# A two-layer transformer kernel in hi/lo float32: P^T one head longer in DRAM, and K and Q of a layer-1 head pair in one 512-column projection

## The chip, the core and the metric

The kernel runs on one core of one Trainium2 chip. The metric is device time in microseconds (us), lower is better. It is given as the median of three runs; one further execution was taken with the hardware profiler, and all rows below are from that one.

Engine names in the profile: PE is the matmul array (TensorE), PEld its weight loads, DVE is VectorE, ACT is ScalarE, POOL is GpSimd, SP is SyncE, whose queue issues all DMAs here.

## What is computed

Two transformer layers on x of shape (2, 512, 512), all in float32. Layer 0: attention with 32 query heads of width 128 that share 8 K/V heads, rotary embedding and a causal mask, then a feed-forward that is one linear map with eight low-rank additions. Layer 1: attention with 32 heads, biases, and a root-mean-square norm on Q and K, without a mask, then a gated feed-forward with low-rank additions. Every block is wrapped as x = x + LN(block(LN(x))):

```python
# layer 1 attention
q = rmsnorm((x @ Wq + bq).reshape(b, n, H, HD), gq)
k = rmsnorm((x @ Wk + bk).reshape(b, n, H, HD), gk)
v = (x @ Wv + bv).reshape(b, n, H, HD)
scores = einsum('bnhd,bmhd->bhnm', q, k) / sqrt(HD)
out = einsum('bhnm,bmhd->bnhd', softmax(scores), v) @ Wo + bo
```

## The kernel before

**Exact products from pairs.** Each float32 operand of a matmul is split into a high and a low part of the type fp32r (hi is a copy, lo = x - hi), and `mm3` adds three products: hi hi, hi lo, lo hi. So each operand costs a copy (ScalarE or VectorE) and a subtraction (GpSimd or VectorE), and each product three matmuls.

**Units and heads.** The work of a layer is cut into units: a head pair p of one batch b. A unit has two heads (j = 0, 1); the list `heads` numbers them. For each head TensorE has: the scores (four query tiles of 128 x 512), the product with V (`av`), and shares of the unit's projections of Q, K and V and of the output projection (`out_proj`, accumulated into y in SBUF).

**Order of issue.** The program is written out by a list scheduler that runs while the program is built. The items of TensorE stand in streams: `main` (scores and, for other units, attention products), "a" (attention products), "q", "v", "o" (fills: Q/K projections, V projections, output projections). Each item has a nominal place `nom` in `main` and a condition; `streams` takes a fill when its place has come, or, up to `ahead` places early, when `main` waits. The work of the other engines hangs on the items as generators, whose stages are issued when a modelled clock says so; `pick` gives an operation to the engine that would finish it first by fixed costs. On the chip each engine then runs its instructions in that order, held by semaphores. Since every instruction passes through one helper, all of them bear line 102 in the profile: they are told apart by tile names and shapes.

**Memory.** The large tiles share an arena of 37 slots of 4 KB a partition ("ar" in the profile); a tag (W for weights, P, T, PT, pt, qk, ot, v, nat, ...) takes a half or a whole slot, and `NBUF`, changed by `PHASES` at five places of the work, bounds how many of a tag may live. `room` says whether a tile fits; `wait` is a stage that waits for it, first come first served. PSUM tiles are ps_pj (projections), ps_s (scores), ps_oy (attention and output products), ps_tr (transposes).

**P^T.** In most units (`lag`) P is transposed not by TensorE but as 32 x 32 blocks on VectorE into T (in `softmax_tail`), stored to DRAM (pc in layer 0, pd in layer 1) and read back by four DMAs into PT with the blocks in place; from PT a copy and a subtraction make the pieces pt (hi, lo) of 256 queries by 128 keys, which `av_items` consumes. DRAM has three such buffers; the products of a head stand in `main` one head after its scores. The K and Q of a layer-1 unit are transposed in the same way through DRAM (`flip`; kdk and kdq).

**Layer-1 projections.** `l1_weights` loads Wk and Wq of a head pair each in two halves into two W tiles (hi, lo). `proj` makes, for K and then for Q, four row tiles of 128 x 256; two of them share a PSUM tile, to which VectorE adds the bias. A square (ScalarE) and a sum (VectorE) give the norm; K is scaled by it, and Q's factor rq is applied in the exponential:

```python
nc.vector.tensor_reduce(m, ps, AX.X, ALU.max, negate=True)
nc.vector.tensor_tensor(mr, m, r, ALU.mult)
```

**Weights ahead.** `LEAD` says how many units before its use a weight starts to load. Units near the ends of a layer (`CUT`) run batch by batch with weights of their own.

Of the kernel before, what the change touches and what calls it, by code (L numbers as in the profile page):

```python
# [30 lines left out]
LAT = 0.1  # L31
FIRST = "x0 x1 x2 k x3 q r v y o z"
# [24 lines left out]
class Item:  # L57
    """a piece of TensorE's work, to be issued when cond holds"""
# [5 lines left out]
class Engine:  # L64
    """An engine that keeps its order of issue, with a clock (us) of its work."""
# [58 lines left out]
class Engines:  # L124
    WEIGHT = dict(vector=1.0, scalar=0.5, gpsimd=0.0)

    def pick(self, *cands):
        """issue the one of the candidates (engine, op, args...) that is done first"""
# [21 lines left out]
    def mul(self, out, a, s):  # L150
        """by a factor of each row"""
        self.pick(("gpsimd", "tensor_scalar", out, a, s, 1.0, ALU.mult, ALU.mult),
                  ("vector", "tensor_scalar", out, a, s, None, ALU.mult),
                  ("scalar", "activation", out, a, AF.Copy, dict(scale=s)))

    def copy(self, out, a):
        """from PSUM"""
# [9 lines left out]
class Kern:  # L167
    """Work is written as items: functions, or generators that yield the time
    (of TensorE's work) after which their next stage is to be issued."""
# [3 lines left out]
                m=6, mr=6, rs=6, ri=6, st=6, mv=10, ve=8, r=10, c=8, r8=6, rq=4,  # L173
# [43 lines left out]
    # the large tiles: a half or the whole of a slot each (halves of one type only in a slot)  # L217
# [3 lines left out]
    def room(self, tag, n, dt=None):  # L221
        if self.live.get(tag, 0) + n > self.NBUF[tag]:
            return False
        free = sum(not u for u in self.used)
        if self.HALF[tag] == 2:
            return n <= free
# [69 lines left out]
    def phase(self, i):  # L296
        """what is tuned for each phase of the work"""
# [27 lines left out]
    def wait(self, tag, n=1):  # L325
        """in a stage: until n slots are free, first come first served"""
# [7 lines left out]
    def low(self, eng):  # L334
        """in a stage of low priority: until the engine has nothing issued to it"""
# [9 lines left out]
    def streams(self, main, fills, bg):  # L345
        """Issue the streams of items, each in its order: a fill when its nominal place in
        main has come, or main waits; bg starts at its nominal place."""
# [30 lines left out]
    def pe(self, t):  # L378
        """t: at the full clock, which TensorE has after a busy tick only"""
# [13 lines left out]
    def mm3(self, out, pairs, start=True, stop=True):  # L393
        """exact hi/lo products: hi hi + hi lo + lo hi"""
# [11 lines left out]
    def setup(self):  # L406
# [10 lines left out]
        self.pd0 = [[self.dr.tile([P, 4, 2, 64 * (h + 1)], F32, name=f"pc{i}{h}") for h in range(2)] for i in range(3)]  # L417
        self.pd = [self.dr.tile([P, 2, 4, 256], F32, name=f"pd{i}") for i in range(3)]
        self.kd = {n: [self.dr.tile([P, 4, 256], F32, name=f"kd{n}{i}") for i in range(2)] for n in "kq"}
        self.ready = {}  # L420
        self.ident = cp.tile([P, P], F32, name="ident")
# [7 lines left out]
    def consts(self):  # L429
# [5 lines left out]
        nc.vector.scalar_tensor_tensor(self.g, self.gqk[:, 0:1], SCALE, self.gqk[:, 1:2], ALU.mult, ALU.mult)  # L435
# [6 lines left out]
    def split(self, hi, lo, raw):  # L442
        """hi + lo = raw exactly"""
# [105 lines left out]
    def resid(self, b, tt, lvl):  # L549
        """x of level lvl + 1 = x + LN(y); returned short of a constant of each row"""  # L550
# [10 lines left out]
        if lvl == 3:  # L561
# [10 lines left out]
            nc.sync.dma_start(self.xsrc(b, tt, 4), x)  # L572
            self.rel(x)
# [6 lines left out]
        def store():  # L580
# [8 lines left out]
            nc.sync.dma_start(self.xsrc(b, tt, lvl + 1), xo)  # L589
            self.rel(xo)  # L590
# [3 lines left out]
    def boundary(self, b, tt, lvl):  # L594
        """from the finished y of level lvl on"""
# [21 lines left out]
    def out_proj(self, b, first, last, ot, w, badd, lvl):  # L617
        """y += O Wo over the heads of this unit"""
# [415 lines left out]
    def l1_pre(self, hp, b, w, lag):  # L1034
# [4 lines left out]
        def proj(i, n, tt):  # L1039
# [11 lines left out]
            if z == 0:  # L1051
                return
# [630 lines left out]
```

## Time and profile before

| | |
|---|---|
| median of 3 runs | 2111.2 us (2106.71 to 2113.66) |
| span of the profiled execution | 2117.8 us (no time of that execution beyond its span is listed) |
| mean granted TensorE clock | 0.993 |
| TensorE busy | 2056.7 us, 97% |
| VectorE, GpSimd, ScalarE busy | 1801.4, 1446.3, 1337.7 us |
| DMA | 370.54 MB, mean 175 GB/s |
| instructions | 41211 |

By stage, from the windows: layer 0's attention runs to about 650 us, layer 0's feed-forward and the norms around it to about 750, layer 1's attention to about 1890, layer 1's feed-forward to the end. "Busy" of an engine is the time in which at least one of its instructions was under way; matmuls overlap, so one that is listed with 283 ns follows the one before it much sooner. The chain of work that ended last merges runs of instructions, and the length of such a run divided by its count is the step from one matmul to the next.

### The profile page before, as it was taken

To read this page: it belongs to the slowest core of one execution; us is meant where nothing else is said; L and a number is where in the kernel's file an instruction comes from. 1 tells how busy PE (TensorE), PEld (TensorE's weight loads), DVE (VectorE), ACT (ScalarE), POOL (GpSimd) and SP (SyncE) were. 2 spreads that over 40 slices of the span, in tenths; PEclk is the share of its full clock that TensorE was granted. 3 is DMA by queue.
4 is the path that set the end of the run, shared out by engine and by line. 5 is a ranking of instruction groups with operands and counts; after the bars stand their busy time and mean duration, and the time that the engine had idled before them with its cause. 6 is when DMAs were issued, how large, how long until landed. Compare 5 with 4: busy or idle time off the path is not lost.

```text
span 2117.8 us, 41211 instructions
## 1 busy us (share of the span) xinstructions
PE 2056.7 (97%) x12605; PEld 1827.5 (86%) x12605; DVE 1801.4 (85%) x4210; ACT 1337.7 (63%) x3247; POOL 1446.3 (68%) x1786
## 2 busy tenths in 40 slices
PE   8999999999999999999999999999999999989998
PEld 7888888888888798889899999999999898977886
DVE  7998899899888889889889999899989988888534
ACT  5776677577766668776666666666667666664212
POOL 5686678688875567877677777777777776774212
PEclk9999999999999999999999999999999999999999
DMA  2476567577652235887877777777777787763021
GB/s 98 127 183 166 145 185 183 143 200 199 177 159 66 71 103 166 244 232 223 227 202 229 220 227 211 207 221 219 225 206 232 213 240 212 224 178 93 31 67 44
DMA packets 476566, 370.54 MB, mean 175 GB/s; under 512 B 117400, under 2 KB 424488, under 8 KB 476344
## 3 DMA queue, kind: packets, MB, share of 16 engines
q1 hardware_dynamic: 476344, 367.91, 60.9%
q8 instruction: 99, 1.62, 0.3%
q14 instruction: 123, 1.01, 0.2%
HBM read 232.12 MB, written 135.66 MB: 174 GB/s over the span
## 4 chain that ended last, share of the span: by engine, by line
PE 54%; DMA 12%; DVE 9%; SPq 3%; issue 2%; POOL 2%; ACT 2%; DVEq 0%; ACTq 0%; POOLq 0%
PE ps_pj L102 23%; PE ps_oy L102 19%; PE ps_s L102 10%; DVE ar L102 6%; SPq L102 3%; DMA pd<-ar 3%; DMA ar<-pd 2%; POOL ar L102 2%; DMA kdk<-ar 2%; ACT ar L102 2%; DMA ar<-kdq 2%; DMA kdq<-ar 2%; PE ps_tr L102 1%; DMA ar<-pc 1%; DVE m L102 1%
## 5 line engine op out<-in xcount | busy, mean ns | idle before, releaser
L102 POOL TENSOR_TENSOR ar<-ar,ar 128x256 fp32r<-128x256 f32 (+4 forms) x1223 | 1058.3, 887 | 456.6 <-ACT ar L102 333.6
L102 PE MATMUL ps_oy<-ar,ar 128*128 128x256 f32 (+2 forms) x4014 | 832.2, 342 | 28.7 <-DVE ar L102 14.0
L102 PEld LDWEIGHTS ps_oy<-ar,ar 128*128 128x128 f32 x4014 | 653.5, 190 | 133.1 <-DVE ar L102 22.5
L102 ACT CAST ar<-ar 128x256 fp32r<-128x256 f32 (+3 forms) x1166 | 531.5, 490 | 305.4 <-DMA ar<-pd 117.1
L102 PE MATMUL ps_pj<-ar,xh 128*128 128x256 f32 (+1 forms) x3392 | 635.2, 285 | 0.9 <-POOL ar L102 0.6
L102 PEld LDWEIGHTS ps_pj<-ar,xh 128*128 128x128 f32 x3392 | 536.0, 190 | 14.5 <-POOL ar L102 1.1
L102 PE MATMUL ps_pj<-ar,xl 128*128 128x256 f32 (+1 forms) x1696 | 482.9, 285 | 0.0
L102 DVE STREAM_TRANSPOSE ar<-ar 128x256 f32<-128x256 f32 (+3 forms) x688 | 347.9, 533 | 16.9 <-DMA pd<-ar 9.7
L102 DVE TENSOR_TENSOR ar<-ps_pj,ar 128x512 f32<-128x512 f32 (+2 forms) x448 | 305.4, 683 | 52.5 <-PE ps_pj L102 44.8
L102 PE MATMUL ps_s<-ar,ar 128*128 128x512 f32 (+2 forms) x1252 | 338.5, 376 | 8.6 <-DVE ar L102 4.7
L102 PEld LDWEIGHTS ps_pj<-ar,xl 128*128 128x128 f32 x1696 | 322.9, 190 | 2.1 <-DVE xl L102 0.7
L102 PE MATMUL ps_pj<-xh,ar 128*128 128x512 f32 x816 | 286.6, 399 | 0.7 <-ACT xh L102 0.7
L102 DVE TENSOR_TENSOR y<-ps_oy,y 128x512 f32<-128x512 f32 x272 | 184.8, 680 | 81.8 <-PE ps_oy L102 80.2
L102 PEld LDWEIGHTS ps_s<-ar,ar 128*128 128x128 f32 x1252 | 214.5, 189 | 44.0 <-DVE ar L102 12.6
L102 DVE TENSOR_TENSOR ar<-ar,ar 128x256 fp32r<-128x256 f32 (+5 forms) x328 | 207.9, 652 | 51.1 <-ACT ar L102 50.1
L102 ACT ACTIVATE ar<-ps_s,mr,rq 128x512 f32<-128x512 f32 x256 | 198.6, 777 | 46.7 <-DVE mr L102 36.9
L102 PEld LDWEIGHTS ps_pj<-xh,ar 128*128 128x128 f32 x816 | 154.0, 189 | 31.7 <-ACT xh L102 1.1
L102 DVE TENSOR_REDUCE m<-ps_s 128x1 f32<-128x512 f32 x256 | 170.9, 673 | 6.2 <-PE ps_s L102 5.0
L102 ACT ACTIVATE ar<-ar,ri 128x512 f32<-128x512 f32 (+3 forms) x245 | 149.6, 621 | 38.3 <-DVE ri L102 37.1
L102 POOL TENSOR_SCALAR ar<-ar,ri 128x512 f32<-128x512 f32 (+3 forms) x202 | 133.0, 661 | 54.3 <-DVE ri L102 48.9
L102 PE MATMUL ps_pj<-xl,ar 128*128 128x512 f32 (+1 forms) x408 | 161.2, 395 | 0.0
L102 ACT ACTIVATE ar<-ps_s,m 128x512 f32<-128x512 f32 (+3 forms) x256 | 133.8, 526 | 23.4 <-DVE m L102 14.8
(91 smaller groups left out, 2105.5 us busy)
## 6 DMA issues: line engine op xcount, KB each, us to landing
pd<-ar SPq DMA_DIRECT2D x240, 256.0 KB, 3.7
ar<-pd SPq DMA_DIRECT2D x480, 128.0 KB, 3.3
ar<-pc SPq DMA_DIRECT2D x200, 128.0 KB, 3.0
ar<-in_wq SPq DMA_DIRECT2D x86, 256.0 KB, 4.1
ar<-in_wo SPq DMA_DIRECT2D x86, 256.0 KB, 3.6
kdk<-ar SPq DMA_DIRECT2D x31, 512.0 KB, 4.8
ar<-kdk SPq DMA_DIRECT2D x124, 128.0 KB, 4.0
kdq<-ar SPq DMA_DIRECT2D x31, 512.0 KB, 5.1
```

The source lines that it names most:

```text
L102: r = self.k.tc.keep_in_program_order(f(*args, **kw))
```

## The change

- P^T of a lagged unit is consumed two heads after its scores, not one (`pend`), the output projection one head later, and there are five DRAM buffers, not three. Layer 1's loads from DRAM and its copies out of PT keep the order of their use (`turn`, `place`); a head waits for its DRAM buffer's last reader (`loads`).
- K and Q of a layer-1 head pair have one weight array `wkq1` of 512 columns, loaded in four quarters, one bias array, and one matmul of 512 columns for each chunk and product. The items stand half a head earlier (`EARLY`). The norm's factors are made for two row tiles at a time.
- Layer-1 scores: g carries the sign, and one pass over the scores applies Q's factor and takes the minimum.
- `room` leaves two slots free when a W, v, nat or raw tile is asked for. The last feed-forward's weights wait until the last Wo is loaded (`wlast`). Two stores release their tile a stage later.
- Comments and docstrings are taken out. `PHASES` is as before; rq goes from 4 to 8.

```diff
+EARLY = 0.5
...
         free = sum(not u for u in self.used)
+        if tag in ("W", "v", "nat", "raw"):
+            free -= 2
...
-        self.pd0 = [... for i in range(3)]
-        self.pd = [... for i in range(3)]
+        self.pd0 = [... for i in range(5)]
+        self.pd = [... for i in range(5)]
...
+        head = st["head", j]
+        while self.loads.get(head - 5, 2) < 2:
+            yield 0.1
+        self.loads.setdefault(head, 0)
         yield from self.wait("T")
...
+        o = 1 - h if st["causal"] else h
+        while not st["causal"] and self.turn[0] < st["place", j] + o:
+            yield 0.1
         yield from self.wait("PT")
+        self.turn[0] = max(self.turn[0], st["place", j] + o + 1)
         pt = self.t("PT", [P, 4, 256])
         for b in range(4):
             nc.sync.dma_start(pt[32 * b:32 * b + 32, :, :n], d[:, b, :].rearrange("(a k) c -> k a c", a=4))
-        yield
+        self.loads[head] += 1
+        yield
+        while not st["causal"] and self.turn[1] < 2 * head + o:
+            yield 0.1
...
-            bqk = self.t("bqk", [P, 2, 256])
-            for i, n in enumerate(("bq", "bk")):
-                self.bcast(bqk[:, i, :], a[n][hp * 256:(hp + 1) * 256])
-        early = [bias] + [self.load_w(a["w" + n + "1"][hp], [P, NC, 256], w, n) for n in "kq"]
+            bkq = self.t("bqk", [P, 512])
+            self.bcast(bkq, a["bkq"][hp * 512:(hp + 1) * 512])
+        def quarter(c):
+            if c % 2 == 0:
+                yield from self.wait("W", 2)
+                box[c // 2] = (self.t("W", [P, 2, 512], F32R), self.t("W", [P, 2, 512], F32R))
...
+            self.nc.sync.dma_start(raw, a["wkq1"][hp][:, c:c + 1, :])
...
+            if box["n"] == NC:
+                w["kq"] = [box[0], box[1]]
+        early = [bias] + [lambda c=c: quarter(c) for c in range(NC)]
...
-            self.mm3(pj[:, z, :], [(self.xh[b][:, c, sl], self.xl[b][:, c, sl], w[n][0][:, c, :], w[n][1][:, c, :])
-                                   for c in range(NC)])
+            self.mm3(pj.rearrange("p n d -> p (n d)"),
+                     [(self.xh[b][:, c, sl], self.xl[b][:, c, sl], w["kq"][c // 2][0][:, c % 2, :], w["kq"][c // 2][1][:, c % 2, :])
+                      for c in range(NC)])
...
-            nc.vector.tensor_tensor(nat[:, ts, :], pj, bias, ALU.add)
+            for i, n in enumerate("kq"):
+                nc.vector.tensor_tensor(st["nat" + n][:, tt, :], pj[:, i, :], w["b"][:, i * 256:i * 256 + 256], ALU.add)
...
-            nc.scalar.activation(sq, nat[:, ts, :].rearrange("p t (h d) -> p (t h) d", h=2), AF.Square)
+            for i, n in enumerate("kq"):
+                nc.scalar.activation(sq[:, 2 * i:2 * i + 2, :], st["nat" + n][:, tt, :].rearrange("p (h d) -> p h d", h=2),
+                                     AF.Square)
...
-        early = [pq(1, "k", t) for t in range(4)] + [pq(0, "q", t) for t in range(4)]
+        early = [Item(lambda t=t: proj_ok(t), lambda t=t: proj(t)) for t in range(4)]
...
-            nc.vector.tensor_reduce(m, ps, AX.X, ALU.max, negate=True)
...
-            nc.vector.tensor_tensor(mr, m, r, ALU.mult)
...
-            yield from self.softmax_tail(st, j, qt, ps, mr, r, S)
+            nc.vector.tensor_scalar(ps, ps, r, 3.0e38, ALU.mult, ALU.min, accum_out=m)
+            yield
+            yield from self.softmax_tail(st, j, qt, ps, m, -1.0, S)
...
+                    while "o" not in self.wlast:
+                        yield 0.5
                     yield from self.wait("W", 2)
...
-            pre(n)[2]["slot", j] = i % 3
+            pre(n)[2]["slot", j] = i % 5
...
+                if n > 1 and lag[n - 2] and lag[n - 1]:
+                    fill["o"] += post(n - 2)
...
-                if n > 0 and lag[n - 1]:
+                if n and lag[n - 1] and not lag[n]:
                     fill["o"] += post(n - 1)
...
-            if i and lag[heads[i - 1][0]]:
-                todo += av_lag(*heads[i - 1])
+            while pend and (len(pend) >= 2 or not lag[n]):
+                todo += av_lag(*heads[pend.pop(0)])
+            if lag[n]:
+                pend.append(i)
...
-                    x.nom = x.nom or base + 2 + k * m / len(xs)
+                    x.nom = x.nom or base + 2 + k * m / len(xs) - (EARLY * m if L and f == "q" and len(xs) == 4 else 0)
```

## The prediction

> **What bounds the kernel now.** I read the page's engine shares and clock row first, then busy time by stage, then the chain of waits and the timeline of TensorE, last the groups by shape.
>
> Part 1 of the page and the clock row of part 2 (engine, busy us, share, instructions; one digit per 1/40 of the span):
>
> ```profile
> PE 2056.7 (97%) x12605; PEld 1827.5 (86%) x12605; DVE 1801.4 (85%) x4210; ACT 1337.7 (63%) x3247; POOL 1446.3 (68%) x1786
> PEclk9999999999999999999999999999999999999999
> ```
>
> TensorE is the bound: 61 us of the span are idle. So a change pays only by fewer TensorE microseconds or by filling some of those 61. The windows say where they are (window, length, PE busy, PEld, DVE, ACT, POOL, clock, DMA share, GB/s):
>
> ```profile
> 50.00:600.00 550.00, 544.59 (x2975) 475.02 (x2974) 489.60 (x1308) 380.06 (x1094) 411.17 (x494) 1.00 0.64 170
> 600.00:750.00 150.00, 144.52 (x796) 120.18 (x795) 126.24 (x321) 99.65 (x252) 94.74 (x125) 1.00 0.29 92
> 750.00:1050.00 300.00, 288.28 (x1933) 261.27 (x1933) 263.76 (x583) 211.53 (x466) 220.38 (x276) 0.99 0.68 200
> 1050.00:1700.00 650.00, 644.97 (x4530) 598.26 (x4529) 592.48 (x1315) 422.99 (x974) 486.72 (x587) 1.00 0.76 218
> 1700.00:1900.00 200.00, 186.04 (x1216) 169.47 (x1214) 168.04 (x384) 132.24 (x294) 147.41 (x184) 0.96 0.76 217
> ```
>
> Idle: 5.4 (layer 0), 5.5 (between the layers), 11.7 (start of layer 1), 5.0 (650 us of steady layer 1), 14.0 (its end). The rest lies in the first 50 us and after 1900, which the change hardly touches. VectorE, at 90% in steady layer 1, comes next.
>
> What those gaps are, in TensorE's timeline (start, length, instruction, count, idle before and what ended it):
>
> ```profile
> 1871.63 0.51 PE L102 MATMUL ps_oy<-ar,ar 128*128 128x256 f32 x2 [0.97 <-POOL ar L102]
> ...
> 1876.43 0.63 PE L102 MATMUL ps_oy<-ar,ar 128*128 128x256 f32 x2 [1.50 <-POOL ar L102]
> ```
>
> 256-column products into ps_oy are O^T = V^T P^T over a piece of P^T: TensorE waits until GpSimd has made its low part. In the waits of all engines ps_oy comes first on TensorE: 14.0 us on VectorE, 8.5 on GpSimd, 5.6 on ScalarE.
>
> The price of the projections, from the chain that ended last (start, length, count):
>
> ```profile
> 1328.10 2.88 PE ps_pj L102 x24
> 1500.72 2.87 PE ps_pj L102 x24
> 1911.56 2.72 PE ps_pj L102 x12
> 1944.85 2.78 PE ps_pj L102 x12
> 1959.91 2.77 PE ps_pj L102 x12
> ```
>
> The first two are K/Q pieces of 256 columns, 0.120 us each; the others 512-column products of the last stage, 0.227 to 0.232 us.
>
> **The change part by part.** *Projection.* One layer-1 unit (head pair, batch) now runs 4 row tiles x 4 chunks x 3 products for K and again for Q: 96 matmuls of 256 columns, 96 x 0.120 = 11.5 us. After: 48 of 512, by the middle piece 48 x 0.231 = 11.1 us. The saving, 0.44 us, times 32 units is 14 us, on the path, since steady layer 1 leaves TensorE 0.8% idle. The Trainium skill's page "TensorE: Matmul & The Clock Gate", section "Back-to-back issue gap", speaks against most of it: columns/2.4 plus 2.5 ns, so 109 and 216 ns, and a unit would save 0.13 us, 4 us in all. I take the trace's 14 and keep 4 as the weak end; 20, with the shortest 512 piece (2.72), is the other.
>
> *Scores of layer 1*, 256 of them: the maximum (673 ns) and its product with the row factor (365 ns) become one pass over PSUM that scales, writes back and reduces. No such instruction is in the trace; the nearest row is layer 0's masked reduction, 128x512, 700 ns, with its accumulator read, 137 ns. VectorE saves (1038-837) x 256 = 51 us; if it cost two full passes (1373 ns) it would lose 86, and if the read were free it would save 87. I take 51. The exponential loses its per-row scale: 777 to 686 ns (layer 0's row), 23 us of ScalarE.
>
> *Bias and squares*: 128 bias additions of 682 ns become 256 of half the size, by layer 0's 256-column row 415 ns: VectorE +19 us. 128 squares of 630 ns become 256 at about 402 (the 256-column cast): ScalarE +22 us. The sum reductions, the 64 reciprocal roots on GpSimd and the K scalings keep their count. Net VectorE -32 us, ScalarE 0. None of it is counted in the sum: TensorE covers it, and losing that cover (the two-pass case) would add 105 us over the 1100 of layer 1, VectorE would go from 91% to 100%, and some 15 us could be lost.
>
> *Weights*: 21 sets come as four quarters of 128x512 instead of four halves of 2x256; loads stay 84, and 42 bias loads become 21. Low parts: 168 GpSimd subtractions of 769 ns become 84 of 1309, -19 us of GpSimd. But projection now starts when all four quarters and both nat tiles are there; before, K needed its own two. The old set is released about half a head later (a layer-1 unit, two heads, takes 34 us: in the chain such a piece comes at 1466.87 and at 1500.72), which leaves about one head to load the next; a set's loads land in 4.1 to 4.6 us and its casts (0.6 us) and subtractions pipeline behind. Zero in the steady part.
>
> *P^T rests a head more.* Per head, 8 pieces (layer 1) or 5 (layer 0) are consumed one head later. Moved with them: the eight loads from DRAM, their casts and subtractions, and the output projection (by one head). On the SP queue the load is no longer issued at once behind the store: today SP stands 212.8 us, 105 times, on stores of pd, and weight loads and K/Q stores queue behind. ScalarE stands 117.1 us on the loads themselves, and casts, then GpSimd's subtractions, queue behind that. With a head of slack both should mostly go; they are not TensorE time. On TensorE I credit half of the attention gaps: the waits of each window put 5.1 us (layer 0), 8.4 (start of layer 1) and 11.1 (its end) on ps_oy, 24.6 together, so -12. Half, because a piece can only be cast when a pt slot (5 to 7) is free, so the extra time is in DRAM, not in finished pieces. Ends: 0 and -24.
>
> *The clock.* 1700-1900 shows 0.96, 8 us lost. The same page, section "What's actually happening", makes the clock fall only after an idle window of some 3.4 us; the longest wait of TensorE there is 2.2 us. By the page, shorter gaps change nothing; by the trace, a stretch rich in small gaps does lose clock, so fewer gaps recover some: -2 of the 8.
>
> *Fill.* The first head of each lagged stretch already has no attention product; now two have none. Layer 1: 24 x 0.12 = 2.9 us of TensorE work put off; layer 0 about 1.8, an estimate from the same step per column. If nothing fills in, +4.7; a head's VectorE work (0.91 x 17 = 15 us) exceeds what is left, so I take +3.
>
> *Longer lives.* V, Wo and full PT and pt slots stay a head longer in the same arena, weights must leave two slots free, P^T loads and casts keep an order, and the last feed-forward's weights wait for the last Wo. These waits are made while the program is written out: they move an instruction's place and hold up nothing by themselves on an engine's queue. K's chain (squares, root, scaling, transposes, 4.8 us to DRAM, 4.0 back, scaling, casts) starts when both projections end, later than now, but EARLY moves the projection half a head forward. Together between 0 and +40; I take +5, mostly for 1700-1900, where the last wait falls. Two small ends: four more zeroing DMAs (2.4 to 2.8 us to landing) near 70 us beside a busy TensorE, 0; some tiles released a step later, 0.
>
> Sum: -14 -12 -2 +3 +5 = -20, of which I give back 2 for steady-state gaps not foreseen: -18. The profiled execution spans 2117.8 us, so 2099.8; no time around it is listed. The median of the runs, 2111.2, is 6.6 below that span, so in their terms 2093.
>
> **The rivals.** *Weights too late (slower).* Place: 1700-1900, where units carry weights of their own and DMA is already at 0.76. Held slots plus the two kept free starve the W tiles, and the feed-forward's w1 and w3 start a head later than today. For: the idle and the low clock are there already. Against: steady layer 1 consumes 8 W tiles per pair over four heads, 67 us. It decides when w1/w3 of the first unit are not split as the last scores end, near 1890: one head of delay (17 us) with a half-speed restart, plus as much again spread over starved heads and the layer boundary, is +40 on -14: 2137.
>
> *Nothing but the columns.* If pt slots alone set when a piece is ready, the rest buys nothing and the change does not do what it says: -14 + 3: 2100.
>
> *A draw.* The skill's 4 us of columns, eaten by the fill: 2111.
>
> **How the numbers follow.** Measurement can tell about 0.3%, 6.3 us, from no change. Main case 0.42 at 2093, own range 2075 to 2104; columns only 0.16 at 2100; draw 0.11; weights late, or another starved stage, 0.31, between 2118 and 2160. Faster is 0.58, same 0.11, slower 0.31. The range 2072 to 2133 leaves out about 0.04 below and 0.15 above.
>
> **What would show it.** Right: ps_pj from 256 to 512 columns at about 0.231 us; 256 tensor products of one element (mr) gone; ps_oy waits of TensorE under 15 us; ScalarE's wait for pd loads far below 117; steady layer 1 shorter by 0.4 us a unit. Wrong: longer gaps in front of ps_pj or ps_s, ended by weight casts or K's chain; clock below 0.99 in more stretches; VectorE over 95%.

## The result, and the profile after

The changed kernel takes 2135.1 us (median of 4 runs, 2130.6 to 2136.5) where the kernel before took 2112.4 on the same chip (2106.7 to 2116.5): ratio 1.0109, 95% interval 1.0089 to 1.0129. It is slower by some 23 us; the forecast was 18 us faster.

The profiled execution spans 2133.4 us against 2117.8. That difference, 15.6 us, is what the traces can account for. The time of a run of after is some 2 us longer than its span (2135.2 for the profiled execution), so this profile is an execution at the median. If the same 2 us hold for the kernel before, its profile is an execution some 7 us slower than its median. Where these 7 us lie is not known, so every difference from the trace of before carries an uncertainty of that size.

The page of after: span, part 1 and the clock row.

```profile
span 2133.4 us, 38147 instructions
PE 2048.7 (96%) x11069; PEld 1756.4 (82%) x11069; DVE 1703.9 (80%) x4188; ACT 1375.8 (64%) x3476; POOL 1457.8 (68%) x1751
PEclk9999999999999999999999999999999999999999
```

TensorE has 1536 matmuls less and is busy 8.0 us less, but its idle time has grown from 61.1 to 84.7 us. That is the whole 15.6: +23.6 idle, -8.0 busy. VectorE lost 97 us of work and is at 80%. TensorE has less work, and more than twice as much was lost in waits.

Windows of after (window, length, PE, PEld, DVE, ACT, POOL busy, clock, DMA share, GB/s), the ones shown of before:

```profile
50.00:600.00 550.00, 550.00 (x3017) 481.26 (x3016) 490.92 (x1308) 395.09 (x1145) 428.03 (x514) 1.00 0.65 174
600.00:750.00 150.00, 141.72 (x744) 116.76 (x743) 119.41 (x305) 95.01 (x239) 86.05 (x109) 1.00 0.28 87
750.00:1050.00 300.00, 280.10 (x1498) 237.79 (x1497) 242.55 (x591) 207.46 (x485) 221.09 (x261) 0.97 0.67 193
1050.00:1700.00 650.00, 637.31 (x3616) 553.05 (x3615) 519.18 (x1289) 448.88 (x1115) 495.93 (x574) 1.00 0.76 219
1700.00:1900.00 200.00, 181.14 (x994) 155.50 (x992) 163.11 (x382) 133.03 (x319) 141.53 (x171) 0.95 0.74 216
```

Idle now, with before in brackets: 0.0 (5.4) in layer 0, 8.3 (5.5) between the layers, 19.9 (11.7) at the start of layer 1, 12.7 (5.0) in steady layer 1, 18.9 (14.0) at its end. Of the attention stages, only layer 0's gained.

The five largest waits of TensorE, before and then after (engine, what, releaser: total us, times, longest):

```profile
PE ps_oy L102 <- DVE ar L102: 14.0, 17, 2.2
PE ps_tr L102 <- ACT ar L102: 11.4, 7, 7.3
PE ps_oy L102 <- POOL ar L102: 8.5, 14, 1.5
PE ps_oy L102 <- ACT ar L102: 5.6, 7, 1.6
PE ps_s L102 <- DVE ar L102: 4.7, 15, 0.5
```

```profile
PE ps_tr L103 <- ACT ar L103: 22.3, 10, 6.8
PE ps_oy L103 <- POOL ar L103: 17.8, 19, 3.7
PE ps_oy L103 <- DVE ar L103: 11.9, 11, 2.3
PE ps_s L103 <- POOL ar L103: 8.0, 11, 1.3
PE ps_oy L103 <- ACT ar L103: 5.7, 7, 1.3
```

The attention waits (ps_oy) were to fall from 28.1 us below 15; they rose to 35.4, and half of them now end with GpSimd. Transposes of norms and feed-forward (ps_tr, on ScalarE) rose from 11.4 to 22.3.

What such a ps_oy wait is, in the timelines of GpSimd and, last line, TensorE (start, length, instruction, count, idle before):

```profile
918.46 1.12 POOL L103 TENSOR_SCALAR ar<-ar,g 128x1024 f32<-128x1024 f32 x1 [0.75 <-DMA ar<-kdk]
919.54 1.27 POOL L103 TENSOR_TENSOR ar<-ar,ar 128x512 fp32r<-128x512 f32 x1
920.77 1.65 POOL L103 TENSOR_TENSOR rq<-r,neg 128x8 f32<-128x8 f32 x1
922.39 3.56 POOL L103 TENSOR_TENSOR ar<-ar,ar 128x256 fp32r<-128x256 f32 x3
...
923.16 0.80 PE L103 MATMUL ps_oy<-ar,ar 128*128 128x256 f32 x2 [3.71 <-POOL ar L103]
```

The low part of a P^T piece (the 128x256 subtractions) stands in GpSimd's queue behind three instructions of K's chain, 4.0 us together, and TensorE stands 3.71 us. P^T had rested a head longer in DRAM. Its pieces were still made at the last moment. A piece can be made only when a pt slot is free; whether that is what held these up is tested below.

The groups of VectorE that the change made (shape and count, busy us, mean ns, idle before):

```profile
L103 DVE TENSOR_SCALAR_CACHE_REDUCE ps_s<-ps_s,rq 128x512 f32<-128x512 f32 x256 | 186.8, 739 | 13.5 <-PE ps_s L103 13.1
L103 DVE TENSOR_TENSOR ar<-ps_pj,ar 128x256 f32<-128x256 f32 x256 | 96.5, 418 | 163.8 <-PE ps_pj L103 153.2 <-POOL ar L103 9.3 <-issue 1.0
L103 DVE DVE_READ_ACCUMULATOR ps_s<-ps_s,rq 128x1 f32 x256 | 35.1, 137 | 0.0
```

Their prices were estimated well (837 ns taken for the pass with its read, 876 measured; 415 for the half bias addition, 418 measured), and none of it is on the path.

Where the time goes, by moments read from the two traces (us, before then after; "head n" is the first pass of VectorE over the scores of the n-th head of layer 1, the norm is handed over when ScalarE casts its last tile of xh, and a first output is VectorE's first write to y from the feed-forward's products):

| moment | before | after | difference |
|---|---|---|---|
| head 0 | 772.4 | 748.1 | -24.3 |
| head 4 | 859.3 | 872.1 | +12.8 |
| head 20 | 1129.0 | 1133.0 | +4.0 |
| us a unit, heads 20 to 52 | 34.48 | 34.27 | -0.21 |
| last score | 1892.6 | 1888.1 | -4.5 |
| norm of batch 0 handed to the feed-forward | 1895 | 1910 | +15 |
| first output of the feed-forward, batch 0 | 1940 | 1956 | +16 |
| the same, batch 1 | 1996 | 2015 | +19 |
| end | 2117.8 | 2133.4 | +15.6 |

A unit of steady layer 1 is shorter by half of the 0.44 us that was forecast (the order of issue alone moves it as much, see *b_lat* below), the start of the layer gives that away, and at the last score the kernel is still 4.5 us ahead. The stretch from the last score to the end is 20 us longer. The loads of the last feed-forward's weights, one group of before and one of after (count, issue time in ns, first to last start):

```profile
L102 SPq DMA_DIRECT2D ar<-in_w x14: 340/415/467, 1856.0 to 1920.6; - x14
```
```profile
L103 SPq DMA_DIRECT2D ar<-in_w x14: 341/385/499, 1888.8 to 1929.6; - x14
```

They start 33 us later. And TensorE, in its timeline, waits for batch 0's norm, its first feed-forward product coming at 1913.91. The product before, then the wait and the product after:

```profile
1901.13 0.47 PE L102 MATMUL ps_pj<-xh,ar 128*128 128x512 f32 x1
```
```profile
1894.44 1.12 PE L103 MATMUL ps_tr<-ident,ar 128*128 128x128 f32 x4 [6.71 <-ACT ar L103]
...
1913.91 0.39 PE L103 MATMUL ps_pj<-xh,ar 128*128 128x512 f32 x1
```

### The profile page after: what moved, and what is told of

The parts are those of the page before. It is cut to its first block, busy times and chain, and to the rows that moved or that the text cites. A ratio compares the mean times of both kernels' runs of the same rounds, so it can differ in the third digit from the quotient of the medians.

```text
span 2133.4 us, 38147 instructions
## 1 busy us (share of the span) xinstructions
PE 2048.7 (96%) x11069; PEld 1756.4 (82%) x11069; DVE 1703.9 (80%) x4188; ACT 1375.8 (64%) x3476; POOL 1457.8 (68%) x1751
## 4 chain that ended last, share of the span: by engine, by line
PE 73%; DVE 8%; DMA 8%; POOL 4%; issue 2%; SPq 2%; ACT 1%; POOLq 0%; DVEq 0%; ACTq 0%
PE ps_pj L103 32%; PE ps_oy L103 26%; PE ps_s L103 13%; DVE ar L103 5%; POOL ar L103 3%; DMA ar<-pd 2%; PE ps_tr L103 2%; SPq L103 2%; DMA ar<-kdk 1%; DMA kdq<-ar 1%; DMA ar<-in_wkq 1%; ACT ar L103 1%; DVE ps_s L103 1%; POOL rq L103 1%; DMA pd<-ar 1%
## 5 line engine op out<-in xcount | busy, mean ns | idle before, releaser
L103 POOL TENSOR_TENSOR ar<-ar,ar 128x256 fp32r<-128x256 f32 (+3 forms) x1220 | 1089.0, 917 | 456.7 <-ACT ar L103 356.6
L103 PE MATMUL ps_oy<-ar,ar 128*128 128x512 f32 (+2 forms) x4014 | 829.7, 342 | 36.1 <-POOL ar L103 17.8
L103 DVE TENSOR_TENSOR ar<-ps_pj,ar 128x256 f32<-128x256 f32 (+3 forms) x576 | 315.6, 567 | 201.4 <-PE ps_pj L103 179.9
L103 PEld LDWEIGHTS ps_pj<-ar,xh 128*128 128x128 f32 x2368 | 403.0, 190 | 45.1
L103 PE MATMUL ps_pj<-ar,xl 128*128 128x256 f32 (+1 forms) x1184 | 395.6, 334 | 0.9 <-DVE xl L103 0.9
L103 ACT ACTIVATE ar<-ps_s,m 128x512 f32<-128x512 f32 (+3 forms) x512 | 308.5, 605 | 61.2 <-DVE m L103 21.2
L103 PEld LDWEIGHTS ps_pj<-ar,xl 128*128 128x128 f32 x1184 | 224.9, 190 | 24.5 <-DVE xl L103 1.3
L103 DVE TENSOR_TENSOR ar<-ar,ar 128x256 fp32r<-128x256 f32 (+4 forms) x252 | 181.8, 734 | 33.9 <-ACT ar L103 33.0
L103 ACT ACTIVATE ar<-ar,ri 128x512 f32<-128x512 f32 (+3 forms) x284 | 175.3, 628 | 40.3 <-DVE ri L103 39.2
L103 DVE TENSOR_SCALAR_CACHE_REDUCE ps_s<-ps_s,rq 128x512 f32<-128x512 f32 x256 | 186.8, 739 | 13.5 <-PE ps_s L103 13.1
L103 DVE CUSTOM_DVE_ANT_0 ps_s<-ps_s,ar 128x512 f32<-128x512 f32 (+3 forms) x256 | 121.9, 488 | 7.5 <-PE ps_s L103 7.4
```

The costliest lines, as they stand in the source:

```text
L103: r = self.k.tc.keep_in_program_order(f(*args, **kw))
```

## The experiments

Two hypotheses came out of this. *The end*: the feed-forward is late because batch 0's last output projection comes a head later and because the weights wait for the last Wo. *The middle*: the columns are saved, but K, which is now finished together with Q, comes late, and P^T's pieces queue with its chain. Rivals: the longer rest alone is the loss; the joint projection alone is; or the order of issue, which every edit reshuffles, is just a worse draw.

Each kernel's ratio is to the kernel before on the same chip (its median lay between 2108.1 and 2115.3), so ratios compare across rows and medians only within a set. "Unit" is us a unit from head 20 to head 52, then the last score and the first feed-forward output of each batch, all of the profiled run.

| kernel | median us | ratio, 95% interval | unit | last score | batch 0 | batch 1 |
|---|---|---|---|---|---|---|
| before | | | 34.48 | 1892.6 | 1940 | 1996 |
| after | 2135.1 | 1.0109 [1.0089, 1.0129] | 34.27 | 1888.1 | 1956 | 2015 |
| b_lat | 2121.9 | 1.0040 [1.0025, 1.0056] | 34.25 | 1884.3 | 1939 | 1995 |
| e3_restonly | 2145.9 | 1.0161 [1.0135, 1.0186] | 35.08 | 1903.2 | 1970 | 2027 |
| e5_cols | 2164.1 | 1.0254 [1.0226, 1.0283] | 36.17 | 1934.9 | 1978 | 2039 |
| e4_l1rest1 | 2139.3 | 1.0125 [1.0101, 1.0148] | 34.50 | 1897.4 | 1952 | 2021 |
| e1_drain | 2140.8 | 1.0145 [1.0109, 1.0181] | 34.30 | 1889.1 | 1944 | 2016 |
| e7_nogate | 2129.9 | 1.0074 [1.0057, 1.0092] | 34.38 | 1889.6 | 1952 | 2007 |
| e8_drain_nogate | 2124.9 | 1.0052 [1.0032, 1.0072] | 34.23 | 1892.1 | 1945 | 2001 |
| pt3 | 2120.9 | 1.0038 [1.0026, 1.0050] | 33.84 | 1863.0 | 1938 | 1997 |
| f2_b_pt3 | 2129.1 | 1.0071 [1.0046, 1.0096] | 34.72 | 1897.9 | 1950 | 2005 |
| f1_pt3_e8 | 2119.7 | 1.0017 [1.0003, 1.0031] | 33.73 | 1875.4 | 1934 | 1989 |
| k2_pt3_nogate | 2106.6 | 0.9995 [0.9976, 1.0015] | 33.67 | 1861.0 | 1920 | 1980 |
| f3_e5_pt3 | 2155.4 | 1.0189 [1.0169, 1.0208] | 35.71 | 1923.0 | 1978 | 2033 |
| f4_e5_early | 2112.6 | 0.9986 [0.9975, 0.9997] | 33.54 | 1873.8 | 1932 | 1988 |
| h3_e5_early15 | 2119.6 | 1.0014 [1.0002, 1.0026] | 33.67 | 1877.0 | 1938 | 1992 |
| h4_mix | 2118.1 | 1.0012 [0.9991, 1.0034] | 33.61 | 1886.4 | 1941 | 1996 |
| h1_early75 | 2136.5 | 1.0099 [1.0074, 1.0124] | 34.03 | 1875.9 | 1940 | 2013 |
| h2_early75_e8 | 2120.0 | 1.0018 [1.0001, 1.0036] | 34.01 | 1884.6 | 1941 | 1997 |
| k1_rest1_early75 | 2115.2 | 1.0028 [1.0009, 1.0047] | 34.23 | 1873.2 | 1929 | 1994 |

**How much the order alone moves.** One constant of the kernel before, the latency with which the order of issue is planned:

```diff
-LAT = 0.1
+LAT = 0.12
```

> The kernel before with one number of the list scheduler's clock changed, LAT 0.12 for 0.1 us: the same work, the same buffers, an order of issue that differs in detail. Theory T (the order before is a lucky one that its settings were fitted to, and any other order of the same work costs 10 us or more): 2120 to 2140. Theory N (the order is not that delicate): 2108 to 2117.

2121.9, ratio 1.0040: in the range of theory T, though 8 us and not the 10 that it named. Nothing of the work changed, and 8 us came from the order. The trace also shows a unit of 34.25 us, as short as in after, and a last score 8 us earlier than before, which its end does not keep (1995 for batch 1, before 1996). So neither after's 0.21 us a unit nor one pair of kernels some 8 us apart says much about an edit; below I lean on larger differences, or on several pairs with one sign. And theory T stays a rival: the two kernels that leave the work of before as it is and move its order (*b_lat*) or its number of slots (*f2_b_pt3*, further down) are slower by 8 and 15 us, so a part of after's 23 can be the loss of an order that suited the kernel before.

**The halves of the change.** *e3_restonly* is the kernel after with K and Q projected by 256 columns each, with the layer-1 scores, the sign of g and rq as in the kernel before; the rest of two heads, the reserve of two slots and the wait for Wo stay. EARLY does not act in it: it holds for four projections a unit, and there are eight again.

```diff
-            self.mm3(pj.rearrange("p n d -> p (n d)"), ... w["kq"] ...
+            self.mm3(pj[:, z, :], ... w[n][0][:, c, :], w[n][1][:, c, :] ...
```

> The changed kernel with layer 1's K and Q projected as before, by 256 columns with weights, bias, norm and scores as before; all of the two-head rest stays. Theory D: the end is as late as in the changed kernel and the 14 us of columns are missing: 2135 to 2150. Theory S: the same. Theory K: the rest alone helps, and without the joint projection the time falls to 2105 to 2115.

*e5_cols* is the reverse: the kernel before with the joint projection, its scores in one pass and EARLY, a rest of one head, no reserve, no wait for Wo.

```diff
-        early = [pq(1, "k", t) for t in range(4)] + [pq(0, "q", t) for t in range(4)]
+        early = [Item(lambda t=t: proj_ok(t), lambda t=t: proj(t)) for t in range(4)]
...
+                    x.nom = x.nom or base + 2 + k * m / len(xs) - (EARLY * m if L and f == "q" and len(xs) == 4 else 0)
```

> The kernel before with the joint K/Q projection alone (weights in quarters, one pass over the scores, items half a head earlier); rest of one head, three DRAM buffers, no slots kept free. Theories D and S: the 14 us of columns, 2095 to 2105. Theory K: slower than before, 2115 or more.

*e4_l1rest1* is the kernel after with layer 1's rest, and its output projection with it, back at one head.

```diff
-            while pend and (len(pend) >= 2 or not lag[n]):
+            while pend and (len(pend) >= (1 if L else 2) or not lag[n]):
```

> The changed kernel with a rest of one head in layer 1 (two heads in layer 0); joint K/Q projection kept. Theories D and S both: the end and the start of layer 1 come back, the columns stay: 2095 to 2105. Theory K: the waits in layer 1 stay, 2125 or more.

Ratios 1.0161, 1.0254 and 1.0125. Theories D and S wanted *e4* and *e5* at 2095 to 2105, K wanted *e3* at 2105 to 2115: each of them fails in one place at least, and each half alone is slower than both together.

*e3* shows what the rest does without the joint projection (the reserve and the wait for Wo are in it too). TensorE's idle time before ps_oy falls from 28.4 us to 17.8 over the whole run, near the 12 that were forecast. But its idle time before scores rises from 8.6 to 30.0, and that before transposes from 12.0 to 22.3. In 1050 to 1700 there is no ps_oy wait left, and this in its place:

```profile
PE ps_s L103 <- POOL ar L103: 12.9, 12, 1.8
```

A unit takes 0.6 us more than before, and the end comes still later. For the joint projection alone, the waits in the same window are these:

```profile
PE ps_s L103 <- POOL ar L103: 15.4, 17, 1.0
PE ps_s L103 <- ACT ar L103: 14.3, 9, 2.1
```

All of its 29.6 us idle there lies before scores. Before, K's four projections came first and Q's behind them, so that K's chain ran under Q's projection. A joint projection ends both at once; that the scores wait for K's last steps on GpSimd and ScalarE for this reason is put to the test with *f4*. With a rest of one head in the kernel after (*e4*) and with two (after), the same window reads:

```profile
PE ps_s L103 <- POOL ar L103: 12.6, 19, 1.0
PE ps_s L103 <- ACT ar L103: 1.7, 3, 1.1
```
```profile
PE ps_oy L103 <- POOL ar L103: 8.5, 11, 1.6
PE ps_s L103 <- POOL ar L103: 3.2, 4, 1.0
PE ps_s L103 <- DVE r L103: 0.7, 1, 0.7
```

So with the joint projection the second head of rest moved TensorE's wait for GpSimd from the scores to the pieces of P^T more than it took it away: 14.3 us idle became 12.7.

**The end.** *e1_drain* takes batch 0's last pairs at one head's rest, and its output projection at the place of before. *e7_nogate* lets the feed-forward's weights load without waiting for the last Wo. *e8_drain_nogate* is both.

```diff
-                if n and lag[n - 1] and not lag[n]:
+                if n and lag[n - 1] and (not lag[n] or n == NA - 2):
...
-            while pend and (len(pend) >= 2 or not lag[n]):
+            while pend and (len(pend) >= (1 if n == NA - 2 else 2) or not lag[n]):
```
```diff
-                    while "o" not in self.wlast:
-                        yield 0.5
```

> The changed kernel, but in the last lagged unit but one of layer 1's end (batch 0's last unit is consumed while batch 1's last lagged unit runs) the rest is one head again, so that the output projection of batch 0's last unit comes a head earlier. Theory D (drain: the loss is the layer norm of batch 0, one head late, with TensorE idle before the feed-forward): first product of the feed-forward back from 1914 to about 1900 us, the 6.7 us gap gone, time about 2120 (-15). Theory S (start of layer 1: the loss is the longer fill at 800 to 950): no change, 2133 to 2137. Theory K (the joint K/Q projection makes the waits): no change either.

> The changed kernel without the wait of the last feed-forward's weights for the last Wo. Theory G (that wait costs: the first of those weights starts to load at 1889 us, before at 1856): loads start near 1860 again, the later gaps before the feed-forward go, 2122 to 2130. Theory D (the layer norm of batch 0 a head late is the limit): the weights come earlier but the first feed-forward product stays at 1914, 2133 to 2137.

> The early drain of batch 0's last unit together with the weights' wait taken away. Theory D+G (each of the two hides the other: the early drain alone moved the first output of the feed-forward to 1944 us but the second batch's still came at 2016): first feed-forward output near 1942 and second batch's near 2000, 2116 to 2123. If only one of them counts, the time equals the better of the two single ones.

The drain alone gained nothing (1.0145, outside all three expectations): batch 0's first output came 12 us earlier, at 1944, but the weights' first load only at 1897.9, and batch 1's output stayed at 2016. Without the wait for Wo 1.0074, as theory G wanted; with both 1.0052, two us above what "each hides the other" asked for. Three pairs differ by the wait for Wo and nothing else: after against *e7* gains 7 us by the ratios, *pt3* against *k2_pt3_nogate* below 9 (1.0038 to 0.9995), and *e1* against *e8*, both with the drain, 20. A fourth, *h1* against *h2* below, takes the drain in as well and gains 17 (1.0099 to 1.0018). One sign throughout: the wait for Wo costs 7 to 20 us, more where the drain is early. The drain has no such record: it gained 5 us in *e8* over *e7*, and lost 8 in *e1* over after and 5 in *f1* over *k2*. The later norm of batch 0 is seen in the trace, but this edit, which hurries the last pairs, does not recover it.

**Slots for P^T's pieces.** If the extra head of rest is idle time in DRAM because pt slots are short, more slots must help the kernel after and leave the one before as it is.

```diff
-    dict(scalar=0.25, ..., pt=5, ...)
-    dict(W=15, ...)
-    dict(W=16, ..., pt=6, ...)
+    dict(scalar=0.25, ..., pt=8, ...)
+    dict(pt=8, W=15, ...)
+    dict(W=16, ..., pt=9, ...)
```

> The changed kernel with three more pt tiles (finished pieces of P^T) in layer 1: 8, 8 and 9 for 5, 5 and 6. Theory B (the longer rest is spent in DRAM because pt tiles are short; a piece is still made just before its product, behind K's scaling, subtraction and root on GpSimd's in-order queue): the 7.8 us of ps_oy waits on GpSimd in steady layer 1 fall below 3 and the time by 5 to 10 us, to 2125 to 2130. Theory K (K's own chain is what is late, ps_s waits): no change, 2133 to 2137. Theory A (the arena is short): slower.

> The kernel before with the same three more slots for P^T pieces from layer 1 on. Theory that the slots are short only because the change lets a head's P^T rest longer: same as before within 5 us (2108 to 2118). Rival, that more slots help any order of this kernel and say nothing on the change: 2095 to 2103, about the 14 us that they gave the kernel after. A third, that the order of issue is disturbed by any setting: 2118 to 2125, as the changed latency alone gave.

> The kernel before with the joint projection of K and Q alone (2164.1) and three more slots for P^T pieces. Theory that the joint projection alone loses its time to the scores, which wait for K scaled, transposed and stored on GpSimd and ScalarE: the slots hardly matter, 2155 to 2168, with TensorE's waits before ps_s unchanged near 30 us in 1050 to 1700. Rival, that the P^T pieces are the shortage here too: 2140 to 2150.

The kernel after gains 15 us (1.0109 to 1.0038), more than theory B asked for. The kernel before loses 15 (1.0071); of its three expectations only that of a disturbed order had the sign, and at 2129.1 it is past that one's range. The joint projection alone gains 14 of its 54 (1.0254 to 1.0189), its waits before scores shrinking from 29.6 to 24.7 us: slots are not its main trouble, as its first theory had it. But it rests one head and gains as much as the kernel after, so the 15 us alone do not prove that the longer rest was short of slots. The trace says more. In *pt3* the window 1050 to 1700 reads:

```profile
1050.00:1700.00 650.00, 646.01 (x3683) 563.36 (x3681) 535.91 (x1280) 465.00 (x1152) 510.39 (x595) 1.00 0.77 223
```

4.0 us idle against 12.7; the ps_oy waits of this stretch are gone, and a unit takes 33.84 us, 0.64 less than before. The last score comes 30 us before that of the kernel before, and yet the end of the trace came only 2 us earlier. *f1_pt3_e8* adds the drain and no wait for Wo, *k2_pt3_nogate* only the latter.

> Three edits on the kernel after: three more slots for P^T pieces from layer 1 on (8, 8, 9 in place of 5, 5, 6), no gate of the feed-forward weights' loads on the output projection's, and batch 0's last pairs drained at one head's rest. Alone, the slots measured 2120.9 (-14 on the kernel after), gate and drain together 2124.9 (-10). Theory that the two losses are separate, one in the P^T pieces of the steady stretch and one at the end: they add, 2135 - 14 - 10 = 2111, and more if the earlier end of attention (22 us with the slots alone, given back at the end) now carries through: 2100 to 2111. Rival, that both measured the same wait: 2119 to 2123.

> The kernel after with three more slots for P^T pieces and no gate on the feed-forward weights, batch 0's last pairs resting two heads as in after. With the slots alone attention's last score ran 30 us before that of the kernel before, and the end only 2 us before. Theory that the gate gives it back: 2106 to 2114. Rival, that the resting last pairs (and the order that any edit reshuffles) do: 2117 to 2123.

*k2* ends level with the kernel before (0.9995) and 24 us below the kernel after by the ratios: its first theory holds, within a hair of its lower bound. *f1*, with the drain as well, measured 1.0017 and 2119.7: not its first theory, by which the gains add up, but within its rival's range. Its last score came 14 us after that of *k2*, which differs by the drain alone, and its end in the trace 9. The slots gain in four pairs of the changed kernel or its half (15 in *pt3* over after, 17 in *k2* over *e7*, 7 in *f1* over *e8*, 14 in *f3* over *e5*).

**When the joint projection is due.** If a late K is what costs the joint projection its gain, a whole head earlier in place of half a head must bring it back.

```diff
-EARLY = 0.5
+EARLY = 1.0
```

> The kernel before with the joint projection alone (2164.1), its four projections of each unit due a whole spacing earlier (EARLY 1.0 in place of 0.5). Theory that a unit's K comes too late for its scores: 2140 to 2155, with less of TensorE's wait before ps_s. Rival, that the K chain is late through the load on GpSimd whatever its start: 2160 to 2170.

> The kernel before with the joint projection alone and EARLY 1.5 (0.5: 2164.1; 1.0: 2112.6). Theory that a score's K must only be there in time, so that what is gained stops once no score waits (none waited in 1050 to 1700 at 1.0): 2108 to 2118. Rival, that earlier is still better: under 2106. Third, that tiles held longer stop the projections: 2120 or more.

*h4_mix* keeps 0.5 for layer 1's first four units:

```diff
- (EARLY * m if L and
+ ((EARLY if n > N0 + 3 else 0.5) * m if L and
```

> The kernel before with the joint projection alone, EARLY 0.5 for the first four units of layer 1 and 1.0 from then on. With 1.0 throughout the first heads of layer 1 ran 12 to 18 us behind the kernel before. Theory that the early due time makes this loss (projections in front of the first heads' products): 2100 to 2108. Rival, that the loss is the joint projection's own, at any due time, since scores wait for all of Q and K's last quarter: 2112 to 2120.

With the joint projection alone and EARLY 1.0, 2164.1 became 2112.6, far beyond either expectation: this one number was worth 57 us by the ratios. TensorE's window 1050 to 1700:

```profile
1050.00:1700.00 650.00, 650.00 (x3730) 569.86 (x3729) 524.83 (x1329) 477.69 (x1164) 494.14 (x571) 1.00 0.77 225
```

No idle time at all, against 29.6 us at EARLY 0.5, and a unit takes 33.54 us: 0.94 less than before, of which the columns account for 0.34 to 0.44 (by the steps given below) and the waits of before, 5.0 us in this window, for some more. At 1.5 (1.0014, between two of its expectations) there is nothing more to be had. *h4* (1.0012) answers that the loss at the layer's start (head 4 comes 17 us behind the kernel before) is not made by the early due time: with 0.5 there it is 18 us. Its cause stays open.

**The same in the kernel after.** EARLY 0.75 in the kernel after, with the end edits, and with a rest of one head in layer 1:

```diff
-EARLY = 0.5
+EARLY = 0.75
```

> The kernel after with its joint projections due three quarters of a spacing early in place of half (EARLY 0.75). Theory that K's chain is late in the kernel after too, and that P^T's pieces queue behind it on GpSimd: 2120 to 2130, with TensorE's waits in 1050 to 1700 shorter than 13 us. Rival, that the longer rest already covers K's lateness and the pieces' slots are the limit: 2132 to 2139.

> The kernel after with EARLY 0.75, and with batch 0's last pairs drained at one head's rest and no gate on the feed-forward weights (the two alone: 2124.9). If due time and end are separate losses: h1's gain and 10 us more, 2110 to 2120. If both only shift one wait: 2122 to 2127.

> The kernel after with rest of one head in layer 1 (two in layer 0 as in after) and EARLY 0.75; at EARLY 0.5 it measured 2139.3 with 34.5 us a unit. Theory that once K is in time the second head of rest only keeps P^T pieces waiting for slots: 33.5 to 33.9 us a unit from head 20 to head 52 (after at 0.75: 34.0), and 2116 to 2130. Rival, that the longer rest is what lets the joint projection go: above 34.2 us a unit and 2132 or more.

*h1* has the total of its rival and the shorter waits of its first theory: the last score comes 12 us earlier than in the kernel after, TensorE's idle time in 1050 to 1700 falls from 12.7 us to 6.0, and all of it is lost at the end, where batch 1's first output comes 73 us behind batch 0's (56 before). With the end edits (*h2*) it is 1.0018, at the edge of its first theory. *k1*, a rest of one head in layer 1, has its last score where *h1* has it (1873.2 and 1875.9), hands over batch 0's norm 17 us earlier (1881, *h1* 1898), and measures 1.0028 against 1.0099. Its 34.23 us a unit are the rival's and its time, just below the range, the first theory's. In this pair, with K due earlier, the second head of rest in layer 1 gains nothing up to the last score, and some 15 us are paid after it. At EARLY 0.5 the same pair does not show that: after and *e4* are 245 and 243 us from the last score to the end, so there the second head cost 3 us at the end and had earned 9 by the last score. How much the second head costs at the end is therefore open.

## Why the prediction was wrong

The steps that failed are "-12" for P^T's rest and "+5" for longer lives. With the fill's +3 they had TensorE's waits shrink by 4 us; they grew by 23.6. What the runs showed in their place: three pt slots and no wait for the last Wo (*k2*) give back 24 us, the whole loss against the kernel before. The order of issue, which by itself moved the kernel before by 8 us, has a part in each such number that was not separated.

- *What bounds it.* Right: TensorE. VectorE's relief of 97 us (32 forecast; the planner also gave fewer subtractions to it) bought nothing, as the sum had it.
- *The columns, -14.* The step of a 512-column matmul is 231 ns and that of 256 columns 119 (medians in after). The trace's price stood, but for a small difference between large numbers: 96 x 119 less 48 x 231 ns is 0.34 us a unit, 11 us in all. The skill's 216 and 109, which its page gives for an isolated matmul, did not stand.
- *EARLY moves the projection half a head forward.* The prediction let this cover K's later end. For the joint projection alone half a head is too little: that cost 54 us (*e5*), and a whole head removes it (*f4*). In the kernel after three quarters of a head (*h1*) brought the last score 12 us forward and the end nothing.
- *P^T rests a head more, -12.* The waits for DRAM did go (ScalarE's 117.1 us on the loads is 2.0, SP's 212.8 on the stores is 10.0). With separate projections TensorE's time before ps_oy fell by 10.6 us (*e3*), so the forecast gap closed; but 21 us came back in front of scores and 10 in front of transposes, a cost that the prediction put at nothing, and *e3* is 34 us slower than before. Why the scores wait there is open. Together with the joint projection the ps_oy waits rose to 35.4 us. The prediction named a reason, "a piece can only be cast when a pt slot (5 to 7) is free", and credited half nonetheless; *pt3* supports it, since with three slots more the ps_oy waits of the steady stretch are gone.
- *Longer lives, +5.* This term was mis-sized. Between the last score and the end the kernel loses 20 us in the trace (*b_lat*, with nothing of the end changed, loses 8). One part is the wait for Wo, which the prediction counted among waits that "hold up nothing by themselves on an engine's queue": 7 to 20 us. The later output projection is another by the trace (batch 0's norm 15 us later, a 6.71 us wait behind it) and by *h1* against *k1*, but no edit took it away cleanly.
- *The rival "weights too late"* had the place (1700 to 1900 and the feed-forward), the sign and nearly the time (2137). Its mechanism holds in part: the loads were 33 us late, but by the wait for Wo, not by starved W tiles. Without that wait and with the two slots still kept free (*e7*) they start at 1859.8, before at 1856.0. The half-speed restart that it counted is in the traces (213 ns for 119, last section). That its sum met the time is luck. What the reserve of two slots costs elsewhere was not tried by itself.
- *The clock, -2.* It fell instead, from a mean of 0.993 to 0.987, with the new waits. That shorter gaps change nothing was the prediction's inference from the page, and the trace of before speaks against it: 1750 to 1800 had 0.93 with no wait of TensorE above 2.2 us (the last section shows the place).
- *The fill, +3.* The start of layer 1 turned a lead of 24 us at head 0 into a lag of 13 at head 4. From head 0 to head 4 the kernel before takes 87 us, after 124, the rest alone 96 (*e3*), the joint projection alone 104 (*e5*; *f4* and *h4* 105 and 106): the two halves add 9 and 17 us and do not make up the 37.
- *The signs to look for.* ps_pj at 231 ns, mr gone, ScalarE's wait gone: right. Steady layer 1 shorter by 0.4 us a unit: half of it, and no more than *b_lat* shows. ps_oy under 15 us: wrong, and it was the one that carried the gain. "Longer gaps in front of ps_pj or ps_s, ended by weight casts or K's chain": present, 8.0 us on GpSimd against 2.2.

What stays open: the 7 us by which the profile of before is slow, the loss at the start of layer 1, why scores wait under the longer rest alone, and how much of each pair's difference is its edit and how much the order. No version beats the kernel before by more than 0.3%: *f4* (0.9986 [0.9975, 0.9997]) and *k2* (0.9995) stand beside it, both about 1.1 to 1.2% below the kernel after.

## What to carry to other kernels

Fusing two products whose results have different deadlines delivers both at the later one; move the fused product forward by the time of the one that it delays, and look at the waits in front of that result's reader before anything is concluded about the saved columns. A wait that a deeper pipeline takes from one reader can come back in front of another that shares the same engine, so count TensorE's idle time over all readers, not the waits that the edit aims at. Ask whether the next stage has buffers to use the slack: here slots paid where time did not. Cost the last unit by itself: what the next stage's weights and norm wait for is paid there. And where each edit reshuffles the order of issue, measure first what a mere reshuffle does.

## What the hardware showed that was not expected

- The granted clock of TensorE is not read from idle time or the longest wait alone. Window 1850 to 1900 of *h1* and then of *k2*:

```profile
1850.00:1900.00 50.00, 43.54 (x228) 38.30 (x228) 41.91 (x96) 29.03 (x62) 26.37 (x37) 0.83 0.48 136
```
```profile
1850.00:1900.00 50.00, 42.46 (x218) 34.03 (x218) 42.78 (x94) 34.64 (x71) 27.06 (x40) 0.97 0.40 113
```

  TensorE is busy 43.5 and 42.5 us, its longest wait is 4.1 and 4.6 us, and the clock is 0.83 and 0.97. In after the same window has 40.3 us busy, a longest wait of 6.7 us, and 0.83. What the mean consists of is seen in the steps of the 256-column matmuls: in *h1* they are 213 ns, not 119, from 1850.7 to 1859.7 (between waits at first) and from 1882.9 to 1886.3, in *k2* only from 1868.5 to 1871.7.
- Waits that are short one by one can go before such a stretch. In before, TensorE's timeline has four waits in 5 us, none above 1.5, 3.5 us together:

```profile
1781.01 0.38 PE L102 MATMUL ps_oy<-ar,ar 128*128 128x256 f32 x1 [0.52 <-ACT ar L102]
1781.82 0.51 PE L102 MATMUL ps_oy<-ar,ar 128*128 128x256 f32 x2 [0.42 <-POOL ar L102]
1783.78 0.38 PE L102 MATMUL ps_oy<-ar,ar 128*128 128x256 f32 x1 [1.46 <-ACT ar L102]
1785.28 0.79 PE L102 MATMUL ps_oy<-ar,ar 128*128 128x256 f32 x2 [1.11 <-DVE ar L102]
```

  From 1785.7 to 1791.2 its matmuls of 256 columns then follow each other by 213 ns (119 elsewhere) and those of 512 by 427 (231).
- A pass that scales, writes back and reduces 128x512 in PSUM takes 739 ns, 66 ns more than the plain maximum of the kernel before (673), and 137 ns more to read its accumulator.
